# Small loads on GpSimd's queue, ten groups in flight, and gates kept in PSUM in a planned graph-network kernel

## The chip, the cores and the metric

The kernel runs on one core of a Trainium2 chip. Its time is the device time of one execution in microseconds (us), and the time before is the median of three runs. A core has five engines that run side by side, each with its own queue of instructions taken in order: TensorE (PE: matrix multiplication; PEld: its weight loads), VectorE (DVE), ScalarE (ACT), GpSimd (POOL) and SyncE (SP), which here only issues transfers (DMAs). SBUF is the working memory. PSUM is the memory that TensorE writes to, in eight banks of 128 partitions x 512 float32 numbers.

## The reference, cut to what matters

```
x: (64, 256, 128)    adj: (256, 256)    weights of 128 x 128 or multiples
x = layernorm(x + sum over k of adj^k x W0[k])       # layer 0: powers 0 to 3, each of two stacks
x = layernorm(x + adj (x W1) + b1)                   # layer 1
x = layernorm(x + norm(adj + I) x W2^T + b2)         # layer 2
h = x                                                # layer 3: a gated recurrence
for step in range(5):
    m  = adj h                                       # in and out matrices are both adj
    av = [m, m];  u = h U3^T + u3_b
    z  = sigmoid(av W3^T + w3_b + u)
    r  = sigmoid(av W4^T + w4_b + u)
    c  = tanh(av W5^T + w5_b + (r h) U5^T + u5_b)    # the candidate
    h  = (1 - z) h + z c                             # = h + z (c - h)
x = layernorm(x + h)
```

Every multiplication is float32.

## The kernel before, in words

The 64 batches are handled in 32 groups of two (`NB`). A group's data is a tile of 128 partitions x 512 numbers. Each group goes through the four layers as a long chain of small operations, and several groups are in flight at once, so that one group's matmuls run while others wait for VectorE, ScalarE, GpSimd or a DMA. Names in the profile are those of the values: `x`, `pmq`, `py` in layer 0; `pm`, `m`, `py`, `yb` in layers 1 and 2; and in step s of the recurrence `pmg`, `mg` (the product with adj), `pr` and `ph` (PSUM banks), `r`, `z`, `hv` (the gates and the candidate), `rh`, `d` = hv - hT, `e` = z d, `hT` (the new state, transposed). The state is then turned into `h` by a VectorE transpose (`th`) and a round trip through DRAM (`dh`, `h`). `pmg`, `pm` and `pmq` are multiplications of 256 x 256 blocks done with seven products instead of eight (`seven`): GpSimd makes the differences `ts` and `tq`, TensorE multiplies in four parts (first, middle, more, rest), ScalarE and VectorE add the blocks up.

Nothing of the order is written by hand. `record` of each group hands every operation to a `Plan`, with its engine, an estimated cost, a lag until the result can be used, and a rank. `Plan.order` then goes through time: on each engine it takes the operation that could start first, and among those that could start together the one of lowest rank. It also gives out the buffers: `slots` says how many there are of each kind (8 PSUM banks, 60 tiles of kind w, and so on), and a value gets a slot at its first use and gives it back after its last. What comes out is one fixed list of instructions for each engine. The rank of a group is its number; for the last `LEVEL` groups it grows with the number of operations the group has already recorded, so that they advance side by side. `ACTIVE` is the number of groups in flight: a group's first operation waits for the last operation of the group `ACTIVE` before it.

The first `HEAD` = 4 batches (two groups) turn x on TensorE (`ptx`), since nothing else is ready yet; the other groups turn it on VectorE (`tx`) and through DRAM (`dx`, `xT`). The last `END` = 8 batches (four groups) turn the final state back on TensorE (`pth`); the others on VectorE (`tn`) and through DRAM (`dn`, `hn`). Then comes the last layernorm: `s` (the sum), `st` and `mv` (statistics on VectorE), `ve`, `nm`, a power on GpSimd (`rs`), and the scaling `y` on ScalarE (lines 475 to 497 and 536 to 545), and the store.

Before the groups, `pre` and `load` (lines 214 to 221) add the operations that prepare constants: `ident` (an identity matrix made by GpSimd), 14 warm-up transposes on TensorE, the transpose and the square of adj, `w0s` (summed and centred by `w0m`), `wb` (the weight of layer 1 and the two biases, centred by `wbm`), the `s_` block sums, and `braw` and `bsum` (the biases of the recurrence). All their loads are issued on SP. The block sums and the centring run on VectorE ahead of the groups' first transposes of x.

The matmul helper is line 198, so every product and block product shows as L198 in the profile. The gates are line 691, the elementwise operations of the recurrence line 698.

Of the kernel before, what the change touches and what calls it, by code (L numbers as in the profile page):

```python
# [13 lines left out]
P = 128  # L14
NB = 2
ACTIVE = 8
HEAD = 4
LEVEL = 5
END = 8
STEPS = 5  # L20
# [136 lines left out]
def kernel(  # L157
# [39 lines left out]
    def mm(o, lhsT, rhs, start, stop, shared=False):  # L197
# [3 lines left out]
              "ve": [P, Q], "rs": [P, Q]}  # L201
    slots = {"bank": BANKS, "x": ACTIVE + 3, "w": 60, "th": 8, "q": 8, "dram1": 8, "dram2": 16, "st": 12, "mv": 12, "ve": 24, "rs": 12}
    plan = Plan(slots)
# [9 lines left out]

    def pre(rank, engine, cost, run, reads=(), writes=()):
        lag = {"SP": 2300, "PE": 260, "DVE": 260, "ACT": 130, "POOL": 100}[engine]
        plan.add(engine, cost, lag, rank, run, reads, writes)

    def load(rank, name, shape, src, keep=True):
        v = constant(name, shape) if keep else Val("w", shape, name)
        pre(rank, "SP", 450, lambda: nc.sync.dma_start(v.ap, src), [], [v])  # L220
        return v
# [140 lines left out]
    wb, wbm = constant("wb", [P, 3, C]), constant("wbm", [P, 3])  # L362
    pre(1.3, "SP", 450, lambda: nc.sync.dma_start(wb.ap[:, 0, :], w1), [], [wb])
    for i, b in ((1, b1), (2, b2)):
        pre(1.4, "SP", 450, lambda i=i, b=b: nc.sync.dma_start(
            wb.ap[:, i, :], bass.AP(tensor=b.tensor, offset=b.offset, ap=[[0, P], [1, C]])), [wb], [wb])
    pre(0.35, "DVE", 1100, lambda: centre(wb, wbm), [wb], [wb, wbm])
    w1c, b1c, b2c = ((wb, wb.ap[:, i, :]) for i in range(3))
    raw = {name: load(1.5, f"raw_{name}", [P, src.shape[1]], src, False)
           for name, src in (("w2", w2), ("w4", w4_w), ("w3", w3_w), ("w5", w5_w), ("u3", u3_w), ("u5", u5_w))}  # L370
# [29 lines left out]

    def biases():
        for i, src in enumerate((w3_b, w4_b, w5_b, u3_b, u3_b, u5_b)):
            nc.sync.dma_start(braw.ap[:, i:i + 1], src.rearrange("(p o) -> p o", o=1))

    pre(2.5, "SP", 2200, biases, [], [braw])
    pre(0.4, "DVE", 150, lambda: nc.vector.tensor_add(bsum.ap, braw.ap[:, :3], braw.ap[:, 3:]), [braw], [bsum])
# [26 lines left out]
    class Group:  # L433
# [33 lines left out]
        def act(self, run, reads, writes, cost=None, joint=False):  # L467
            return self.add("ACT", cost or act_cost(self.width), 130, run, reads, writes, joint)

# [4 lines left out]

        def statistics(self, tag, s):
            st, mv, ve, rs, nm = (self.val(k, n + tag) for k, n in (
                ("st", "st"), ("mv", "mv"), ("ve", "ve"), ("rs", "rs"), ("ve", "nm")))

            def stats():
                for q in range(self.q):  # L480
                    nc.vector.bn_stats(st.ap[:, q * 6:(q + 1) * 6], nat(s)[:, q, :])  # L481

            def aggr():
                for q in range(self.q):
                    nc.vector.bn_aggr(mv.ap[:, 2 * q:2 * q + 2], st.ap[:, q * 6:(q + 1) * 6])
                mean, var = (mv.ap.rearrange("p (q k) -> p k q", k=2)[:, k] for k in range(2))
                nc.vector.tensor_scalar(ve.ap, var, EPS, None, op0=OP.add)
                nc.vector.tensor_scalar(nm.ap, mean, -1.0, None, op0=OP.mult)

            def scales():  # L490
                nc.gpsimd.tensor_tensor(rs.ap, ve.ap, half[:, :self.q], op=OP.pow)
                nc.gpsimd.tensor_tensor(mv.ap[:, :self.q], nm.ap, rs.ap, op=OP.mult)

            self.dve(stats, [s], [st], 195 * self.q)
            self.dve(aggr, [st], [mv, ve, nm], 67 * self.q + 240)
            self.add("POOL", 1420, 100, scales, [ve, nm], [rs, mv])
            return mv, rs

        def spread_of(self, tag, s):

            y, ve, rs = self.val("w", "y" + tag), self.val("ve", "ve" + tag), self.val("rs", "rs" + tag)

            def squares():
                for q in range(self.q):
                    nc.scalar.activation(nat(y)[:, q, :], nat(s)[:, q, :], AF.Square, scale=C ** -0.5,  # L505
                                         accum_out=ve.ap[:, q:q + 1])

            def scales():
                nc.gpsimd.tensor_scalar(ve.ap, ve.ap, EPS, None, op0=OP.add)  # L509
                nc.gpsimd.tensor_tensor(rs.ap, ve.ap, half[:, :self.q], op=OP.pow)  # L510

            self.act(squares, [s], [y, ve], 400 * self.q)
            self.add("POOL", 1330, 100, scales, [ve], [ve, rs])
            return y, rs

        def normalise_centred(self, tag, s):
            y, rs = self.spread_of(tag, s)

            def run():
                for q in range(self.q):  # L520
                    nc.scalar.mul(nat(y)[:, q, :], nat(s)[:, q, :], rs.ap[:, q:q + 1])  # L521

            self.act(run, [s, rs], [y], 380 * self.q)
            return y
# [6 lines left out]
        def residual(self, tag, ps, resid, left=lambda v: v.ap, right=lambda v: v.ap):  # L531
            s = self.val("w", "s" + tag)
            self.dve(lambda: nc.vector.tensor_add(right(s), left(ps), right(resid)), [ps, resid], [s])
            return (s, *self.statistics(tag, s))

        def normalise(self, tag, s, mv, rs):
            y = self.val("w", "y" + tag)

            def run():
                for q in range(self.q):  # L540
                    nc.scalar.activation(nat(y)[:, q, :], nat(s)[:, q, :], AF.Identity, bias=mv.ap[:, q:q + 1],
                                         scale=rs.ap[:, q:q + 1])

            self.act(run, [s, mv, rs], [y], 400 * self.q)
            return y

        def propagate(self, tag, h, aTs, ins=None, blocks=False, fast=True):

            if fast and self.nb == 2:
                return self.seven(tag, h, aTs, ins or tiles, blocks)  # L550
            ps, outs = self.val("bank", "pm" + tag), by_block if blocks else None

            def run():
                o, a = (outs or plain)(ps), ins or tiles
                for b in range(self.nb):
                    for kt in range(T):
                        mm(o[b], a(h)[:, b, kt], aTs.ap[:, kt, :], kt == 0, kt == T - 1)

            self.pe(pe_cost(N, self.q), run, [h, aTs], [ps])
            return self.copied("m" + tag, ps)  # L560

        def seven(self, tag, h, aTs, ins, blocks):
# [60 lines left out]
            started = self.pe(pe_cost(P, 1), first, [h, aTs], [ps])  # L623
            kept = self.act(lambda: nc.scalar.copy(row(u, 1), row(ps, 0)), [ps], [u], act_cost(P))  # L624
            self.add("POOL", 830, 100, ts01, [h], [ts])
# [6 lines left out]
            self.dve(post13, [ps, w], [m], 215)  # L632
            self.act(lambda: nc.scalar.copy(o(m, 0), o(ps, 0, False)), [ps], [m], act_cost(P), True)
            self.pe(pe_cost(P, 2), rest, [h, tq, sums], [ps], True)
# [60 lines left out]

        def tensor(self, name, op, a, b, way=lambda v: v.ap, out=lambda v: v.ap):
            t = self.val("w", name)
            self.dve(lambda: nc.vector.tensor_tensor(out(t), way(a), way(b), op=op), [a, b], [t])  # L698
            return t

        def record(self):
            x_ = self.val("x", "x")
            plan.add("SP", 450, 4500 if self.start < HEAD else 2700, self.rank(), lambda: nc.sync.dma_start(nat(x_), self.view(x)), [], [x_],
                     self.load_gate)
# [24 lines left out]
            for t in range(T):  # L729
# [12 lines left out]
                self.pe(pe_cost(2 * C, 2 * self.nb), first, [xT, qT, w01, w0s], [p])  # L742
                self.act(moved, [p], [v], act_cost(self.nb * C))
            for t in range(T):
# [10 lines left out]
                self.pe(pe_cost(self.nb * C, T), second, [v, aT], [py[t]])  # L755
                self.act(summed, [py[t]], [s0], act_cost(self.nb * C))
            y = self.normalise_centred("0", s0)
# [24 lines left out]
            for s in range(STEPS):  # L782
# [8 lines left out]
                self.product(pr, w34T, m, False, True, shared=True)  # L791
                z = self.gate_(f"z{s}", pr, AF.Sigmoid, zb)
                self.product(ph, u5T, rh, False, True)
                hv = self.gate_(f"hv{s}", ph, AF.Tanh, hb)

                d = self.tensor(f"d{s}", OP.subtract, hv, hT)
                e = self.tensor(f"e{s}", OP.mult, z, d)
                if s < STEPS - 1:
# [79 lines left out]
```

## Time and profile before

| | |
|---|---|
| median of three runs | 1366.85 us (1366.57 to 1367.98) |
| the profiled run | 1367.95 us, span of its instructions 1365.1 us |
| PE, DVE, ACT, POOL busy | 98%, 72%, 56%, 55% of the span |
| granted TensorE clock | 0.997 of full speed |
| DMA | 134.42 MB, 98 GB/s on average |
| x load, issue to landing (median) | 3.2 us |

The profile is one execution recorded by the hardware. A page gives each engine's busy time, the chain of work that ended last (followed back from the last instruction), and the costliest groups of equal instructions. A row of a group reads: line, engine, operation, written tile <- read tiles, shapes, count | busy us in all, mean ns of one | idle time of the engine just before these instructions, and what ended it. A row in order of time reads: start us, length us, engine, line, operation, tiles, count. A float32 product appears as two matmul records.

### The profile page before, as it was taken

Reading aid. Unit: us, or ns where it says so; the run is one execution under the profiler, and the core shown is the slowest. Engines: PE = TensorE matmul, PEld = TensorE weight load, DVE = VectorE, ACT = ScalarE, POOL = GpSimd, SP = SyncE. Lnnn points to the kernel's source line nnn. Section 1 sums busy time; section 2 is a strip of 40 time slices with the busy share of each in tenths; the row PEclk is TensorE's granted clock in tenths of the full one; section 3 lists DMA queues with packets and bytes.
Section 4 is the critical chain, followed back from the end, with each engine's and each line's share of the span. In section 5 each row is a group of like instructions: output and inputs, shape, how many; then the busy total and the mean of one; then the engine's idle time right before and its main releaser. Section 6 shows DMA issues by size and latency. Waiting matters only on the chain.

```text
span 1365.1 us, 21963 instructions
## 1 busy us (share of the span) xinstructions
PE 1335.7 (98%) x6517; PEld 923.9 (68%) x6517; DVE 983.1 (72%) x2335; ACT 763.7 (56%) x2406; POOL 747.0 (55%) x1089
## 2 busy tenths in 40 slices
PE   8999999999999999999999999999999999999996
PEld 7986756677676666677767666766677766755553
DVE  5466777767767877776767777776766776878777
ACT  3675555555655545565565555654656556754444
POOL 3785643464765455555774554654665446843222
PEclk9999999999999999999999999999999999999998
DMA  6222233442334334333332333232433223233232
GB/s 171 63 63 71 84 101 109 123 117 84 96 93 117 98 96 124 109 95 100 109 101 78 109 118 107 86 106 80 129 101 96 85 86 93 88 114 109 79 93 60
DMA packets 269670, 134.42 MB, mean 98 GB/s; under 512 B 176368, under 2 KB 241392, under 8 KB 269552
## 3 DMA queue, kind: packets, MB, share of 16 engines
q1 hardware_dynamic: 269552, 133.03, 33.7%
q8 instruction: 52, 0.85, 0.3%
q14 instruction: 66, 0.54, 0.1%
HBM read 67.05 MB, written 65.54 MB: 97 GB/s over the span
## 4 chain that ended last, share of the span: by engine, by line
PE 89%; DVE 5%; DMA 2%; ACT 1%; issue 1%; POOL 1%; SPq 1%; ACTq 0%; POOLq 0%; DVEq 0%
PE pr L198 28%; PE ph L198 19%; PE pmg L198 18%; PE py L198 15%; PE pm L198 6%; PE pmq L198 3%; DMA x<-in_x_dram 1%; DVE hT L698 1%; DVE d L698 1%; DVE e L698 0%; DMA w_raw<-in_L_gnn_weight_dram 0%; DVE th L672 0%; DVE rh L698 0%; DVE st L481 0%; DMA wb<-in_L_gnn_b_dram 0%
## 5 line engine op out<-in xcount | busy, mean ns | idle before, releaser
L198 PE MATMUL pr<-mg,w435u5T 128*128 128x512 f32 x640 | 323.5, 595 | 2.0 <-ACT r L691 1.4
L583 POOL TENSOR_TENSOR tsg<-h 128x256 f32<-128x256 f32 x128 | 106.9, 835 | 222.4 <-DMA h<-dh 138.6
L691 ACT ACTIVATE r<-pr,bsum 128x512 f32<-128x512 f32 x160 | 109.6, 685 | 151.3 <-PE pr L198 148.1
L698 DVE TENSOR_TENSOR rh<-r,hT 128x512 f32<-128x512 f32 x160 | 123.2, 770 | 77.4 <-ACT r L691 76.8
L691 ACT ACTIVATE z<-pr,bsum 128x512 f32<-128x512 f32 x160 | 109.7, 685 | 107.7 <-PE pr L198 104.4
L698 DVE TENSOR_TENSOR d<-hv,hT 128x512 f32<-128x512 f32 x160 | 118.1, 738 | 69.5 <-ACT hv L691 68.5
L198 PE MATMUL ph<-rh,w435u5T 128*128 128x512 f32 x320 | 163.9, 595 | 1.1 <-DVE rh L698 1.1
L198 PE MATMUL ph<-mg,w435u5T 128*128 128x512 f32 x320 | 163.3, 592 | 0.0
L198 PE MATMUL pr<-hT,w2u3T 128*128 128x512 f32 x320 | 162.7, 592 | 0.0
L198 PEld LDWEIGHTS pr<-mg,w435u5T 128*128 128x128 f32 x640 | 107.1, 191 | 56.2 <-issue 38.2
L691 ACT ACTIVATE hv<-ph,bsum 128x512 f32<-128x512 f32 x160 | 109.4, 685 | 43.3 <-PE ph L198 42.7
L521 ACT ACTIVATE y<-s,rs 128x128 f32<-128x128 f32 x384 | 122.2, 393 | 13.7 <-POOL rs L510 13.3
L505 ACT ACTIVATE y<-s 128x128 f32<-128x128 f32 x384 | 113.8, 302 | 25.5 <-DVE s L528 25.3
L198 PEld LDWEIGHTS pmg<-s_aTp,tsg 128*128 128x128 f32 x768 | 102.8, 191 | 37.2 <-issue 31.1
L698 DVE TENSOR_TENSOR hT<-hT,e 128x512 f32<-128x512 f32 x160 | 123.7, 773 | 1.4
L698 DVE TENSOR_TENSOR e<-z,d 128x512 f32<-128x512 f32 x160 | 121.4, 759 | 1.9
L198 PEld LDWEIGHTS pmg<-aTp,h 128*128 128x128 f32 x512 | 88.2, 197 | 46.6 <-issue 34.9
L621 DVE TENSOR_TENSOR mg<-pmg,usg 128x256 f32<-128x256 f32 x160 | 67.1, 419 | 62.8 <-PE pmg L198 59.5
L198 PE MATMUL pmg<-s_aTp,tsg 128*128 128x128 f32 x768 | 106.6, 275 | 1.2 <-ACT usg L624 1.0
L510 POOL TENSOR_TENSOR rs<-ve,half 128x4 f32<-128x4 f32 x96 | 101.9, 1062 | 8.0
L509 POOL TENSOR_SCALAR ve<-ve 128x4 f32<-128x4 f32 x96 | 24.5, 255 | 141.8 <-ACT y L505 141.8
L198 PEld LDWEIGHTS ph<-mg,w435u5T 128*128 128x128 f32 x320 | 58.7, 190 | 63.6 <-issue 48.5
(170 smaller groups left out, 2846.9 us busy)
## 6 DMA issues: line engine op xcount, KB each, us to landing
dh<-th SPq DMA_DIRECT2D x160, 256.0 KB, 2.0
h<-dh SPq DMA_DIRECT2D x256, 128.0 KB, 2.5
x<-in_x_dram SPq DMA_DIRECT2D x32, 256.0 KB, 3.2
hT<-dh SPq DMA_DIRECT2D x128, 64.0 KB, 2.0
out_dram<-y SPq DMA_DIRECT2D x32, 256.0 KB, 2.4
dx<-tx SPq DMA_DIRECT2D x30, 256.0 KB, 2.5
xT<-dx SPq DMA_DIRECT2D x60, 128.0 KB, 2.6
dn<-tn SPq DMA_DIRECT2D x28, 256.0 KB, 2.0
```

The source lines that it names most:

```text
L198: nc.tensor.matmul(o, lhsT, rhs, start=start, stop=stop, skip_group_check=shared)
L505: nc.scalar.activation(nat(y)[:, q, :], nat(s)[:, q, :], AF.Square, scale=C ** -0.5, accum_out=ve.ap[:, q:q + 1])
L509: nc.gpsimd.tensor_scalar(ve.ap, ve.ap, EPS, None, op0=OP.add)
L510: nc.gpsimd.tensor_tensor(rs.ap, ve.ap, half[:, :self.q], op=OP.pow)
L521: nc.scalar.mul(nat(y)[:, q, :], nat(s)[:, q, :], rs.ap[:, q:q + 1])
L583: nc.gpsimd.tensor_tensor(ts.ap[:, :2 * P].rearrange("p (x c) -> p x c", x=2), ins(h)[:, 1], ins(h)[:, :, 0], op=OP.subtract)
L621: nc.vector.tensor_tensor(o(m, slice(1, 3)), o(ps, slice(1, 3), False), both, op=OP.add)
L691: self.act(lambda: nc.scalar.activation(t.ap, ps.ap, func, bias=bias[1], scale=1.0), [ps, bias[0]], [t], act_cost(self.width) + 100)
L698: self.dve(lambda: nc.vector.tensor_tensor(out(t), way(a), way(b), op=op), [a, b], [t])
```

## The change

It has five parts.

- The loads of the two biases in `wb` and the six of `braw` are issued from GpSimd's queue; the loads of `w1` and the raw weights stay on SP, at an earlier rank. Loads into one tile no longer wait for each other (`joint`). x is loaded at the rank of a group one and a half places earlier.
- `ACTIVE` goes from 8 to 10, with more slots of the kinds w, th and q; `LEVEL` from 5 to 7.
- `END` goes from 8 to 4, so two groups rather than four turn their state back on TensorE; these two scale the last layernorm on VectorE instead of ScalarE, without the negated mean.
- z and the candidate are written by ScalarE over their own PSUM banks (`pr`, `ph`), and z times the difference by VectorE over z.
- The estimated costs and lags of ScalarE's operations (and a few others) that the planner uses are changed.

```diff
-ACTIVE = 8
+ACTIVE = 10
-LEVEL = 5
-END = 8
+LEVEL = 7
+PLAIN = 0
+END = 4
...
-    slots = {"bank": BANKS, "x": ACTIVE + 3, "w": 60, "th": 8, "q": 8, ...
+    slots = {"bank": BANKS, "x": ACTIVE + 3, "w": 64, "th": 10, "q": 10, ...
...
+    def fetch(rank, o, src, v, queue):
+        e, cost = QUEUES[queue]
+        pre(rank, queue, cost, lambda: e.dma_start(o, src), [], [v], lag=3000, joint=True)
...
-    pre(1.3, "SP", 450, lambda: nc.sync.dma_start(wb.ap[:, 0, :], w1), [], [wb])
+    fetch(0.1, wb.ap[:, 0, :], w1, wb, "SP")
     for i, b in ((1, b1), (2, b2)):
-        pre(1.4, "SP", 450, lambda i=i, b=b: nc.sync.dma_start(
-            wb.ap[:, i, :], bass.AP(tensor=b.tensor, offset=b.offset, ap=[[0, P], [1, C]])), [wb], [wb])
+        fetch(0.1, wb.ap[:, i, :], bass.AP(tensor=b.tensor, offset=b.offset, ap=[[0, P], [1, C]]), wb, "POOL")
...
-    pre(2.5, "SP", 2200, biases, [], [braw])
+    for i, src in enumerate((w3_b, w4_b, w5_b, u3_b, u3_b, u5_b)):
+        fetch(0.2, braw.ap[:, i:i + 1], src.rearrange("(p o) -> p o", o=1), braw, "POOL")
...
-            return self.add("ACT", cost or act_cost(self.width), 130, run, reads, writes, joint)
+            return self.add("ACT", cost or act_cost(self.width), 190, run, reads, writes, joint)
...
+            def near():
+                for q in range(self.q):
+                    nc.vector.tensor_scalar(nat(y)[:, q, :], nat(s)[:, q, :], mv.ap[:, 2 * q:2 * q + 1],
+                                            rs.ap[:, q:q + 1], op0=OP.subtract, op1=OP.mult)
...
-            self.act(run, [s, mv, rs], [y], 400 * self.q)
+            if self.start >= B - END:
+                self.dve(near, [s, mv, rs], [y], 257 * self.q)
+            else:
+                self.act(run, [s, mv, rs], [y], 390 * self.q)
...
-            plan.add("SP", 450, 4500 if self.start < HEAD else 2700, self.rank(), ...
+            plan.add("SP", 450, 4500 if self.start < HEAD else 2700, self.rank() - 1.5, ...
...
-                z = self.gate_(f"z{s}", pr, AF.Sigmoid, zb)
+                z = self.gate_(f"z{s}", pr, AF.Sigmoid, zb, False)
...
-                hv = self.gate_(f"hv{s}", ph, AF.Tanh, hb)
+                hv = self.gate_(f"hv{s}", ph, AF.Tanh, hb, False)
...
-                e = self.tensor(f"e{s}", OP.mult, z, d)
+                e = self.tensor(f"e{s}", OP.mult, z, d, into=pr)
```

## The prediction

> **What bounds the kernel now**
>
> I read the page first (busy shares and the chain that ended last), then the busy time by stage, then the groups of instructions, then the rows in order of time where TensorE is not full: the start and the end.
>
> ```profile
> span 1365.1 us, 21963 instructions
> PE 1335.7 (98%) x6517; PEld 923.9 (68%) x6517; DVE 983.1 (72%) x2335; ACT 763.7 (56%) x2406; POOL 747.0 (55%) x1089
> ...
> PE 89%; DVE 5%; DMA 2%; ACT 1%; issue 1%; POOL 1%; SPq 1%; ACTq 0%; POOLq 0%; DVEq 0%
> ```
>
> TensorE is the bound: 98% busy and 89% of the chain. But the ends of its records are modelled, so I also price its work by the spacing of its starts when it runs densely. In the rows in order of time the median spacing is 0.4295 us for a record of 512 columns, 0.216 for 256 and 0.112 for 128. The groups hold 1600, 792 and 4125 such records: 687.2 + 171.1 + 462.0 = 1320.3 us. So 1365.1 - 1320.3 = 44.8 us of the span are not TensorE's work. The stages say where they lie (columns: window, its length, then busy time and instruction count of each engine):
>
> ```profile
> 0.00:40.00 40.00, 33.23 (x187) 29.72 (x188) 19.93 (x65) 16.50 (x55) 15.20 (x30) 1.00 0.65 179
> 40.00:100.00 60.00, 60.00 (x386) 52.64 (x385) 31.77 (x78) 42.09 (x190) 50.77 (x80) 1.00 0.15 43
> 100.00:1300.00 1200.00, 1190.35 (x5746) 812.44 (x5745) 884.18 (x2064) 674.85 (x2101) 663.12 (x952) 1.00 0.35 100
> 1300.00:1340.00 40.00, 40.00 (x166) 23.92 (x165) 30.29 (x62) 17.46 (x35) 10.38 (x19) 1.00 0.30 86
> 1340.00:1366.00 26.00, 12.12 (x40) 5.19 (x38) 16.89 (x67) 12.81 (x27) 7.49 (x10) 0.83 0.18 51
> ```
>
> Summing (start to next start, less the dense spacing) over each stage gives: head, to 40 us, 8.6 and 1.3 before the first matmul; middle, 40 to 1340, 20.2; from 1340 to TensorE's last record 6.0; after it 8.4. They make 44.5, and the rest is rounding. The head's largest part is three waits for x (columns: start, length, engine, line):
>
> ```profile
> 17.46 1.23 SPq L703 DMA_DIRECT2D x<-in_x_dram  x1
> ...
> 25.98 0.46 PE L198 MATMUL pmq<-a2T,x 128*128 128x128 f32 x2 [2.06 <-DMA x<-in_x_dram]
> ...
> 32.39 0.49 PE L198 MATMUL pmq<-a2T,x 128*128 128x128 f32 x2 [0.65 <-DMA x<-in_x_dram]
> 34.53 0.46 PE L198 MATMUL pmq<-a2T,x 128*128 128x128 f32 x2 [1.65 <-DMA x<-in_x_dram]
> ```
>
> The middle's 20.2 us are some 40 short waits, mostly for ScalarE or VectorE results that come a few tenths late. The end is VectorE's: it works almost without a pause from 1349.4 to 1358.9, and after its last row come GpSimd's power, four ScalarE rows and the store.
>
> ```profile
> 1349.96 0.68 DVE L698 TENSOR_TENSOR rh<-r,hT 128x512 f32<-128x512 f32 x1
> ...
> 1358.70 0.17 DVE L488 TENSOR_SCALAR nm<-mv 128x4 f32<-128x4 f32 x1
> ...
> 1360.19 1.65 ACT L541 ACTIVATE y<-s,mv,rs 128x128 f32<-128x128 f32 x4 [0.81 <-POOL mv L492]
> ```
>
> **What the Trainium skill says**
>
> SBUF — State Buffer, "Who interferes with whom": a VectorE instruction with two SBUF inputs and a GpSimd instruction that reads SBUF lock each other out for a whole instruction; with one SBUF input at most it doesn't. The trace agrees:
>
> ```profile
> L698 DVE TENSOR_TENSOR hT<-hT,e 128x512 f32<-128x512 f32 x160 | 123.7, 773 | 1.4
> L698 DVE TENSOR_TENSOR e<-z,d 128x512 f32<-128x512 f32 x160 | 121.4, 759 | 1.9
> L698 DVE TENSOR_TENSOR d<-hv,hT 128x512 f32<-128x512 f32 x160 | 118.1, 738 | 69.5 <-ACT hv L691 68.5
> L528 DVE TENSOR_TENSOR s<-py,yb 128x512 f32<-128x512 f32 x64 | 43.5, 682 | 12.6 <-PE py L198 11.4 <-POOL ts L587 1.1
> ```
>
> The row with a PSUM input takes 682 ns; the three with two SBUF inputs take 738 to 773, though the median of their rows, read one by one, is 690: the mean is raised by a minority that is held up.
>
> ScalarE: Activation LUTs, "Step-by-step: what each stage is for": ScalarE writes PSUM faster than SBUF. No ScalarE row here writes PSUM.
>
> PSUM — Partial Sum Buffer, "Summary: rules for kernel authors": evacuate promptly, since PSUM is tight. The kernel uses all eight banks.
>
> DMA: Bandwidth & Descriptors, "Specifications": first byte about 1 us from GpSimd's queue, 0.6 from SP's. No GpSimd DMA is in this trace.
>
> **The change part by part**
>
> *Head.* Eight loads (two of wb, six of braw) leave SP for GpSimd's queue; they took 1.28 + 1.38 + 0.43 + 0.58 = 3.7 us of SP's issue. The load of b2 stood behind w0p, so wbm waited 3.2 us for it on VectorE with the transposes of x behind it; x_4 and x_6 were issued only at 17.46. Now they go ahead of w0p, and wbm's 1.3 us of VectorE work comes before w0m. From w0_raw's landing (7.75, now some 0.5 later because x_2 is issued first) VectorE has 9.3 us of work to the end of s_aTp, plus wbm 1.3: tx_4 starts at about 18.9 instead of 21.56. The chain tx_4, dx_4, x_8 moves 2.7 us earlier: x_8's wait of 2.1 goes, x_12's 0.7 too. x_14 lands 2.7 earlier, but TensorE asks for it 2.9 earlier too, so its wait stays near 1.8. Gain 2.9. On GpSimd, eight issues of about 1 us (the page's price, an estimate) precede dinv, which slips from 5.4 to about 9.5; ahat's rows on VectorE, moved behind w0m, need it at 11.7. One issue stands ahead of ident, so the 14 warm-up transposes (3.0 us) and p_at start up to 1 us later; TensorE waited 1.1 us for ahat at 9.36, and p_an now stands behind pmq_0, which absorbs that. If GpSimd's issues are slower, the gain drops to 0; if x_14 comes in time, it is 4.5.
>
> *Middle.* Ten groups instead of eight, truer costs, and buffers for them (w 64, th and q 10) only reorder. I counted, in the written order of both programs, how much TensorE work lies between a matmul and the later one that needs its result through another engine. Shares of tight links fall: product to product through one gate of ScalarE, 22 of 160 under 1.2 us before and 3 after; the last block matmul to the product through post2, 20 under 1.0 before and 14 after; the minimum of that link goes from 0.45 to 0.86. The sum of what links lack against their latency falls from 17 to 8 us. The 17 is close to the 18.3 us of waits over 30 ns found in the trace, so I take 9 us off. The long links (gate to next step's h, 5% point 20.8 before, 21.6 after) are covered in both.
>
> *PSUM.* z, hv and e in PSUM give d, e and hT one SBUF input each: from 738, 759 and 773 to about 685, 160 times each, 34 us of VectorE time, all beside TensorE; its worth is in the 9 us. ScalarE's z and hv: gain 0 to 50 ns, I take 0. VectorE's write of e to PSUM has no row: nearest is the 682 of L528, bounds 650 and 750, I take 685. Against it: the bank of pr is now free after hT's add, not after z. From the last u5T matmul to that point the trace of before shows 0.17 plus 2.9 at least, 3.8 median, 5.75 at the 95% point. In the new order the next user of the bank comes 4.0 us of TensorE work later at the least, 4.5 at the 5% point, 6.7 median. That is mostly enough; the overlap costs an estimated 1 us (0 to 6). So the middle gives -8.
>
> *End.* END 4 leaves two groups on the direct path, so two more take the DMA path: two VectorE transposes more (0.70 each) and eight transposes fewer on TensorE (-0.9 us). Two groups normalise on VectorE: four rows of about 0.22 (nearest: L350) instead of 1.65 us on ScalarE, and lose nm and one GpSimd multiply. LEVEL 7 draws seven groups instead of five to the end together. At the spacings of the rows above (0.61 for 512 elements, 0.78 for st, 0.66 for a transpose), VectorE work from the last rh is 8.9 before and 13.4 after: y of group 60, s, st, mv of group 58 all stand there. After that before has 6.2 us to the end (power 1.0, multiply 0.2, ScalarE 1.65, store 3.2, hops), after has 1.1 of power plus 3.25 of store. So 17.75 against 15.1: +2.65. Earlier, from rh of the first of the seven to the last rh, VectorE has 34.7 us of work and TensorE 34.0, so both can't stay full; taking the larger of the two stretch by stretch gives 41, averaging gives 35. I take 38, that is 4 us of TensorE waits where before had 2.2: +1.85. End: +4.5 (+2 to +8).
>
> Sum: -0.9 - 2.9 - 8 + 4.5 = -7.3 on the profiled span. That run took 1367.95; the median 1366.85 is what I subtract from: 1359.6.
>
> **The rivals**
>
> *More gain.* Middle waits nearly close (-14), end +1.5, head -4.5: 1366.85 - 0.9 - 17.0 = 1349. For it: faster VectorE rows also shorten queues, which the link count leaves out. Against it: part of the 20.2 is jitter under 30 ns a row.
>
> *It cancels.* The middle's waits come from queues on VectorE, not from short links, so only 1 to 2 us go, while head and end go as above: 1366.85 - 0.9 - 2.9 - 1.5 + 4.5 = 1366. For it: VectorE is 72% busy in order.
>
> *Slower: the banks of pr and ph.* TensorE, in order, waits for hT's add (and d's read of ph) before its next group may start a bank. Each of 160 steps losing on average 0.125 us costs 20 us: 1359.6 + 1 + 20 - 9 = about 1372, counting the middle gain as lost. It decides from about 46 ns a step (7.3 us). For it: release latencies of 4.5 to 6 us happen in a quarter of the steps. Against it: the smallest distance, 4.0, is already above the latency's median.
>
> *The change doesn't do what it says.* If VectorE rows stay at 738 to 773, the reorder's gain remains; the result is 1 to 3 us worse.
>
> **How the numbers follow**
>
> A difference of 0.2% (2.7 us) is what a measurement of this kernel can tell from none. Forecast (1354 to 1364.1) 0.58; more gain 0.12; cancels (to 1369.6) 0.17; slower 0.13. Faster is 0.58 + 0.12 = 0.70. The range 1351 to 1369 leaves some 0.06 below and 0.14 above; the forecast's own is 1354 to 1364.
>
> **What would show it**
>
> Head: TensorE's waits for x before 40 us fall from 4.4 to about 1.8. PSUM: d, e, hT near 685 ns. Middle: TensorE idle from 100 to 1300 down from 9.7 to about 5. Banks: waits of TensorE's pm, pr or ph for VectorE's hT or d would be the slower rival. End: VectorE full for the last 45 us, its last row y, and over 15 us from the last rh to the end. I am wrong if VectorE's PSUM write is slow (over 750 ns), or if the end costs over 10 us.

## The result, and the profile after

The changed kernel takes 1358.16 us (median of four runs, 1357.06 to 1359.65); the kernel before took 1367.16 in the same measurement. The ratio is 0.9934, 95% interval 0.9917 to 0.9952: faster by 0.7%. That is 9.0 us less, where the prediction had 7.3, and 1.4 us below its 1359.6. The profiled run has a span of 1355.7 us at a granted clock of 0.996, against 1365.1 before.

The page of the changed kernel, its span, busy times and the engines' shares of the chain that ended last:

```profile
span 1355.7 us, 21892 instructions
...
PE 1331.2 (98%) x6509; PEld 922.0 (68%) x6509; DVE 953.2 (70%) x2343; ACT 756.0 (56%) x2398; POOL 678.0 (50%) x1095
...
PE 94%; DVE 3%; DMA 1%; issue 0%; ACT 0%; SPq 0%; POOL 0%; POOLq 0%; DVEq 0%; ACTq 0%
```

TensorE has 94% of the chain instead of 89%. VectorE has 30 us less to do, GpSimd 69 us less, although no instruction of GpSimd's arithmetic was taken out of the groups' steps. By stage (window, length, busy us and count of PE, PEld, DVE, ACT, POOL, then clock and DMA):

```profile
0.00:40.00 40.00, 34.16 (x189) 30.01 (x189) 21.39 (x65) 16.72 (x56) 21.41 (x41) 1.00 0.67 185
40.00:100.00 60.00, 59.90 (x390) 52.53 (x391) 29.81 (x79) 41.25 (x182) 49.74 (x80) 1.00 0.23 68
100.00:1300.00 1200.00, 1197.76 (x5797) 818.83 (x5796) 856.17 (x2062) 673.20 (x2112) 593.28 (x954) 1.00 0.34 99
1300.00:1340.00 40.00, 38.27 (x133) 19.90 (x131) 35.49 (x92) 20.76 (x41) 9.14 (x15) 1.00 0.35 107
1340.00:1356.00 16.00, 1.12 (x4) 0.71 (x4) 10.36 (x50) 4.10 (x10) 4.43 (x6) 0.63 0.30 85
```

From 100 to 1300 us TensorE is idle for 2.2 us; before it was 9.65. At the end the picture turns: after 1340 TensorE does almost nothing while VectorE works for 10 of 16 us.

The same ledger as in the prediction (each TensorE record's distance to the next, less the dense spacing of its size) gives, in us. "Slack" is what a distance has over the dense spacing. The middle reaches from 40 us to 36 us before the span's end:

| | before | after | difference | predicted |
|---|---|---|---|---|
| TensorE's work | 1320.2 | 1319.3 | -0.9 | -0.9 |
| ahead of the first matmul, and slack to 40 us | 1.3 + 8.6 | 2.5 + 6.8 | -0.6 | -2.9 |
| slack in the middle | 20.2 | 8.9 | -11.3 | -8 |
| slack in the last 36 us, and from the last TensorE record to the end | 6.0 + 8.7 | 8.3 + 9.8 | +3.4 | +4.5 |
| sum | | | -9.4 | -7.3 |

Half of what the middle gains, 5.6 us, lies in its last 220 us (256 to 36 us before the span's end): the slack there falls from 6.8 to 1.2.

In the page's groups the step's four 512-column VectorE rows read (busy us, mean ns, then the idle time before and its releaser):

```profile
L714 DVE TENSOR_TENSOR rh<-r,hT 128x512 f32<-128x512 f32 x160 | 125.5, 787 | 71.6 <-ACT r L707 67.5
...
L714 DVE TENSOR_TENSOR d<-ph,hT 128x512 f32<-128x512 f32 x160 | 109.8, 686 | 78.3 <-ACT ph L707 77.3
...
L714 DVE TENSOR_TENSOR pr<-pr,d 128x512 f32<-128x512 f32 x160 | 110.6, 692 | 1.5
...
L714 DVE TENSOR_TENSOR hT<-hT,pr 128x512 f32<-128x512 f32 x160 | 108.6, 680 | 1.7
```

d, e (now `pr`) and hT fell from 738, 759 and 773 ns to 686, 692 and 680. rh, which still reads two SBUF tiles, did not.

### The profile page after: what moved, and what is told of

The parts are those of the page before. It is cut to its first block, busy times and chain, and to the rows that moved or that the text cites. A ratio compares the mean times of both kernels' runs of the same rounds, so it can differ in the third digit from the quotient of the medians.

```text
span 1355.7 us, 21892 instructions
## 1 busy us (share of the span) xinstructions
PE 1331.2 (98%) x6509; PEld 922.0 (68%) x6509; DVE 953.2 (70%) x2343; ACT 756.0 (56%) x2398; POOL 678.0 (50%) x1095
## 4 chain that ended last, share of the span: by engine, by line
PE 94%; DVE 3%; DMA 1%; issue 0%; ACT 0%; SPq 0%; POOL 0%; POOLq 0%; DVEq 0%; ACTq 0%
PE pr L199 30%; PE ph L199 20%; PE pmg L199 18%; PE py L199 15%; PE pm L199 7%; PE pmq L199 3%; DMA x<-in_x_dram 1%; DMA w_raw<-in_L_gnn_weight_dram 1%; DVE st L487 0%; DMA dx<-tx 0%; DVE s L541 0%; DVE rh L714 0%; DVE tx L730 0%; ACT y L529 0%; DVE y L554 0%
## 5 line engine op out<-in xcount | busy, mean ns | idle before, releaser
L599 POOL TENSOR_TENSOR tsg<-h 128x256 f32<-128x256 f32 x128 | 96.4, 753 | 211.5 <-DMA h<-dh 145.0
L707 ACT ACTIVATE pr<-pr,bsum 128x512 f32<-128x512 f32 x160 | 105.6, 660 | 120.7 <-PE pr L199 115.9
L714 DVE TENSOR_TENSOR d<-ph,hT 128x512 f32<-128x512 f32 x160 | 109.8, 686 | 78.3 <-ACT ph L707 77.3
L707 ACT ACTIVATE ph<-ph,bsum 128x512 f32<-128x512 f32 x160 | 105.5, 659 | 63.7 <-PE ph L199 62.9
L529 ACT ACTIVATE y<-s,rs 128x128 f32<-128x128 f32 x384 | 122.1, 392 | 15.4 <-POOL rs L518 14.7
L517 POOL TENSOR_SCALAR ve<-ve 128x4 f32<-128x4 f32 x96 | 22.6, 235 | 214.3 <-ACT y L513 214.2
L513 ACT ACTIVATE y<-s 128x128 f32<-128x128 f32 x384 | 113.7, 301 | 18.4 <-DVE s L536 18.2
L714 DVE TENSOR_TENSOR pr<-pr,d 128x512 f32<-128x512 f32 x160 | 110.6, 692 | 1.5
L627 DVE TENSOR_TENSOR usg<-usg,pmg 128x128 f32<-128x128 f32 x160 | 45.2, 284 | 91.9 <-PE pmg L199 67.2
L714 DVE TENSOR_TENSOR hT<-hT,pr 128x512 f32<-128x512 f32 x160 | 108.6, 680 | 1.7
```

Source lines behind the costliest of these rows:

```text
L599: nc.gpsimd.tensor_tensor(ts.ap[:, :2 * P].rearrange("p (x c) -> p x c", x=2), ins(h)[:, 1], ins(h)[:, :, 0], op=OP.subtract)
L627: nc.vector.tensor_tensor(row(u, 0), row(u, 1), row(ps, 3), op=OP.add)
L707: self.act(lambda: nc.scalar.activation(t.ap, ps.ap, func, bias=bias[1], scale=1.0), [ps, bias[0]], [t], act_cost(self.width) + 100)
```

## The experiments

Each kernel was timed in turn with the kernel before, on one chip; e1 to e4, e5 to e8, e9 to e11 and e12 ran on different chips, so ratios are compared, and a loss or gain in us is the difference of ratios times 1367. Such a difference is uncertain by about 0.2%. The head, middle and end columns are the ledger of the one profiled run of each (head with the time ahead of the first matmul; end with the time after the last TensorE record). A profiled run can lie 2 us from its kernel's median: e5's is 1.9 us above, e3's 1.8, e4's and e8's 2.2 us below. "Lack" is the sum of what the tight links of the written order fall short of. It is a count made from the order that the planner writes, with ties between equally late inputs settled in one fixed way; no trace shows it. It puts the kernel before at 13.3 us and the changed one at 6.2, where the prediction's count said 17 and 8.

| | ratio to before, 95% interval | us | head | middle | end | lack |
|---|---|---|---|---|---|---|
| before | 1 | | 9.9 | 20.2 | 14.7 | 13.3 |
| changed | 0.9934, 0.9917 to 0.9952 | 1358.16 | 9.3 | 8.9 | 18.1 | 6.2 |
| e1 gates in SBUF, planned anew | 0.9962, 0.9949 to 0.9974 | 1361.23 | 9.5 | 13.2 | 17.4 | 5.2 |
| e2 before, with PSUM alone | 1.0024, 1.0014 to 1.0034 | 1369.91 | 10.3 | 22.6 | 14.5 | 17.6 |
| e3 eight groups | 0.9995, 0.9987 to 1.0003 | 1366.09 | 8.8 | 16.6 | 17.8 | 9.9 |
| e4 old costs | 0.9988, 0.9979 to 0.9996 | 1365.50 | 9.5 | 14.9 | 17.8 | 7.8 |
| e5 gates in SBUF, same order | 1.0010, 1.0004 to 1.0017 | 1368.40 | 11.6 | 19.5 | 18.2 | 6.2 |
| e6 old end | 0.9968, 0.9956 to 0.9981 | 1362.60 | 10.5 | 15.5 | 14.6 | 7.7 |
| e7 old head | 0.9930, 0.9916 to 0.9943 | 1358.51 | 11.1 | 8.6 | 17.4 | 6.2 |
| e8 a version from the pieces | 0.9930, 0.9918 to 0.9943 | 1357.92 | 9.3 | 10.2 | 14.7 | 5.6 |
| e9 two lags | 0.9915, 0.9903 to 0.9928 | 1355.74 | 9.5 | 7.1 | 17.8 | 0.5 |
| e10 e9, ident first, END 8 | 0.9905, 0.9892 to 0.9919 | 1354.97 | 10.2 | 7.8 | 15.5 | 0.5 |
| e11 e9 in SBUF, same order | 0.9978, 0.9968 to 0.9989 | 1364.29 | 10.6 | 14.7 | 17.8 | 0.5 |
| e12 r in PSUM too | 0.9907, 0.9890 to 0.9924 | 1355.26 | 11.3 | 6.5 | 16.2 | 1.6 |

Theory A is the prediction's: the order (ten groups, truer costs, more buffers) carries the middle's gain. B: the time freed on VectorE and GpSimd carries it. C: results that stay in PSUM hold the banks longer and are a burden.

**e1, e2: the PSUM part undone, and alone**

```diff
 e1, against the changed kernel:
-                z = self.gate_(f"z{s}", pr, AF.Sigmoid, zb, False)
+                z = self.gate_(f"z{s}", pr, AF.Sigmoid, zb)
-                hv = self.gate_(f"hv{s}", ph, AF.Tanh, hb, False)
+                hv = self.gate_(f"hv{s}", ph, AF.Tanh, hb)
-                e = self.tensor(f"e{s}", OP.mult, z, d, into=pr)
+                e = self.tensor(f"e{s}", OP.mult, z, d)
 e2: the same three lines the other way round, in the kernel before
```

> The changed kernel with z, the candidate and e put back into SBUF; all else stays. Theory A (the order carries the gain: ten groups, truer costs, more buffers): d, e and hT rise from 680-692 ns to 740-775, GpSimd's rows too, but TensorE's middle loses only 0 to 3 us, so 1358 to 1361 us. Theory B (the freed VectorE and GpSimd time carries it): the middle's slack goes from 9 back to about 20 us, 1368 us. Theory C (PSUM results hold the banks of pr and ph longer and are a burden that the ten groups pay for): the middle gets shorter by up to 4 us, 1354 to 1358; walking the written order with the durations of the traces gives an estimate of -3.6 us before any lock on VectorE is counted.

> The kernel before with only the PSUM part added; eight groups, the old costs, buffers, head and end stay. Theory A: d, e and hT fall to about 690 ns and the time falls a little, 1364 to 1367 us. Theory B: most of the middle's gain appears, 1356 to 1360. Theory C: the bank of pr is kept from w4T's product to hT's add, eight groups don't fill the time, and TensorE waits: walking the written order with the durations of the traces gives an estimate of +14 us over the kernel before, so about 1380; the profile would show middle idle of 20 us or more.

Without PSUM the changed kernel loses 0.28%, 3.8 us, of which the middle has 4.3: between A and B. PSUM alone makes the kernel before *slower* by 0.24%, though d, e and hT do fall to 677 to 692 ns. That excludes B by itself. C has the sign of e2 right but not the size (+3.3 us, not +14), and e1's sign wrong; and no wait of TensorE's `pr`, `ph` or `pm` for hT or d is in e2's list of waits. What rises in e2 is the lack of the links, 13.3 to 17.6. The likely reason is that a bank comes free later, so that the planner finds a worse order.

**e3, e4: eight groups, old costs**

```diff
 e3:
-ACTIVE = 10
+ACTIVE = 8
-... "w": 64, "th": 10, "q": 10, ...
+... "w": 60, "th": 8, "q": 8, ...
 e4 (some of nine such places):
-            return self.add("ACT", cost or act_cost(self.width), 190, run, ...
+            return self.add("ACT", cost or act_cost(self.width), 130, run, ...
-            self.act(squares, [s], [y, ve], 295 * self.q)
+            self.act(squares, [s], [y, ve], 400 * self.q)
```

> The changed kernel with eight groups in flight and the old numbers of buffers (w 60, th 8, q 8); PSUM, costs, head and end stay. Theory A: the tight links come back, the middle's slack goes from 9 to 15 to 18 us: 1364 to 1368 us. Theory B: nothing changes, 1357 to 1360. Theory C: eight groups can't cover the longer bank times; the estimate from the written order is +20 us over the changed kernel: about 1378.

> The changed kernel, planned with the old durations and the old ScalarE lag of 130 ns; ten groups, PSUM, head and end stay. Theory A: part of the tight links comes back (product to product through one gate), the middle's slack rises by 2 to 5 us: 1360 to 1363 us. Theory B: no change, 1357 to 1360. Theory C: little change, the estimate from the written order is +1.7 us: 1358 to 1361.

Each takes most of the gain away: e3 loses 0.61% (8.3 us), e4 0.54% (7.4 us), more than any theory gave e4; e3 is as theory A had it. Together with e1 the single losses sum to 19.5 us, where the whole change gained 9: the parts need each other. C's +20 for e3 is refuted; the walk through the written order that I used for it overrates waits for banks and is not a measure to rely on.

**e5: PSUM undone, the order kept**

```diff
-            t = self.val("w", name) if kept else ps
-            self.act(lambda: nc.scalar.activation(t.ap, ps.ap, func, ...), [ps, bias[0]], [t], ...)
+            v = self.val("w", name)
+            t = v if kept else ps
+            t.held = v
+            self.act(lambda: nc.scalar.activation(v.ap, ps.ap, func, ...), [ps, bias[0]], [t, v], ...)
 (and tensor() reads and writes the held tiles in the same way)
```

The planner still believes that the banks are held, so every queue has the same instructions in the same order (the two traces agree); only the places of z, the candidate and e differ.

> The changed kernel in its own written order, instruction for instruction, but z, the candidate and e are written to SBUF. e1 changed the order as well; here only the places of the data differ. If PSUM acts by the lock between VectorE and GpSimd (theory B's part), d, e and hT rise to about 760-780 ns and the middle's slack goes from 8.9 to 12 to 16 us: 1361 to 1365 us. If PSUM acted mainly through the order that the planner finds (theory A), the time stays at 1357 to 1359.5. If PSUM holds TensorE up through the banks (theory C), giving the banks back early makes it faster: 1354 to 1357.

This is the run that moved my view. It is slower than the changed kernel by 0.76%, 10.4 us: the whole gain is gone, more than the 3 to 7 us that were expected of the lock. The middle's slack is back at 19.5 us. The groups show where it comes from:

```profile
L718 DVE TENSOR_TENSOR rh<-r,hT 128x512 f32<-128x512 f32 x160 | 128.2, 804 | 68.0 <-ACT r L709 64.1
...
L718 DVE TENSOR_TENSOR d<-hv,hT 128x512 f32<-128x512 f32 x160 | 120.9, 756 | 71.8 <-ACT hv L709 69.6
...
L718 DVE TENSOR_TENSOR hT<-hT,e 128x512 f32<-128x512 f32 x160 | 125.5, 785 | 1.7
...
L718 DVE TENSOR_TENSOR e<-z,d 128x512 f32<-128x512 f32 x160 | 125.3, 784 | 1.6
```

and in the 1200 us of the middle VectorE is busy 33 us more than in the changed kernel's row above, GpSimd 70 us more:

```profile
100.00:1300.00 1200.00, 1191.92 (x5769) 814.47 (x5768) 889.65 (x2048) 672.84 (x2104) 663.52 (x953) 1.00 0.34 98
```

The means hide what happens. Read row by row, the medians of all four rows are 691 to 693 ns. Of their 640 rows, 261 lie beside no tensor instruction of GpSimd, and none of these lasts 750 ns. Of the 379 that overlap one, 194 last 750 ns or more, the longest 1802. In the changed kernel 254 rows of d, e and hT overlap GpSimd, and the longest takes 700 ns. This is what the Trainium skill's page SBUF — State Buffer, "Who interferes with whom", describes, a lock for a whole instruction when VectorE reads two SBUF inputs, and this pair of traces agrees.

TensorE seldom waits for d, e or hT. It waits for rh, and for mg and m, which stand behind the held rows on VectorE. From the lists of waits (who waited, for whom: us in all, times, longest), first the changed kernel, then e5:

```profile
PE ph L199 <- DVE rh L714: 0.7, 2, 0.5
PE pmg L199 <- DVE mg L633: 0.5, 1, 0.5
...
PE pmg L199 <- DVE mg L633: 1.6, 2, 1.0
PE ph L199 <- DVE rh L718: 1.3, 4, 0.6
PE pr L199 <- DVE mg L637: 1.2, 2, 0.9
```

In the middle the waits listed for VectorE grow from 1.4 to 4.8 us, those for ScalarE from 0.9 to 2.7, and none names d, e or hT. So the held rows act through the queue. e5 also gives back ScalarE's 25 ns on each z and candidate (below); no run separates the two, but VectorE's waits grow more.

**e6: the old end**

```diff
-LEVEL = 7
-END = 4
+LEVEL = 5
+END = 8
-            if self.start >= B - END:      # normalise on VectorE
+            if False:
```

> The changed kernel with the end of before: LEVEL 5, END 8, normalisation on ScalarE in all groups. The prediction's step for the end (+4.5, measured +3.3 between the two traces, less 0.9 for the transposes that come back to TensorE): 1358.2 - 3.3 + 0.9 = 1355.8, plus up to 1.5 us because the middle's order changes with LEVEL: 1355 to 1358. From the last rh to the end some 15 us instead of 18.9. Rival (the two ends are worth the same, the difference of the traces came from how the groups before happened to lie): 1358 to 1360.

Its last 36 us did what was expected: 14.6 us instead of 18.1. The last rh stands at

```profile
1345.78 0.68 DVE L714 TENSOR_TENSOR rh<-r,hT 128x512 f32<-128x512 f32 x1
```

15.1 us before the span's end of 1360.8. But the kernel is slower than the changed one by 4.6 us, since the middle went from 8.9 to 15.5. Up to 873 us TensorE has the changed kernel's instructions in the same order, with the same slack (5.1 us from 40 us on, against 5.2). All that is added comes later, where the edit begins to act; one stretch holds 3.5 us of idle TensorE:

```profile
1000.00:1200.00 200.00, 196.52 (x970) 136.83 (x969) 136.21 (x340) 118.17 (x399) 103.47 (x165) 0.99 0.29 87
```

From 256 to 36 us before the span's end the slack is 8.6 us, against 1.2 in the changed kernel. The kernels before and e2, also with LEVEL 5 and END 8, have 6.8 and 6.1 there. The nine with LEVEL 7 have 0.8 to 3.3, and e10, whose END is 8 too, has 0.8; e8 (LEVEL 5) has 4.0 and e12 (LEVEL 6) 3.0. So the end's part of the change costs 3.5 us in the last 36 and gives back more ahead of them, and the comparison points to LEVEL as what does the latter. No run changes LEVEL alone.

**e7: the old head**

```diff
-    fetch(0.1, wb.ap[:, 0, :], w1, wb, "SP")
+    pre(1.3, "SP", 450, lambda: nc.sync.dma_start(wb.ap[:, 0, :], w1), [], [wb])
... (the loads of b1, b2, the raw weights and braw likewise as before; all on SP)
-            plan.add("SP", 450, 4500 if self.start < HEAD else 2700, self.rank() - 1.5, ...
+            plan.add("SP", 450, 4500 if self.start < HEAD else 2700, self.rank(), ...
```

> The changed kernel with the loads of before: all small loads on SP, in the old places, and x without its lead of 1.5 in rank. The prediction's step for the head (-2.9): undoing it gives 1361. The difference measured between the traces (-0.6: 1.8 less waiting, 1.2 more ahead of the first matmul): 1358 to 1359.5. A rival says that GpSimd's eight loads are a net loss, since they stand ahead of the identity matrix: 1355 to 1358; then the first matmul starts at 1.3 us instead of 2.5 and TensorE's slack up to 40 us stays below 9.3 in total.

No difference: 0.9930 against 0.9934. The waits for x come back, and the first matmul starts earlier:

```profile
1.34 3.25 PE L247 MATMUL warm<-ident 128*128 128x128 f32 x14 [1.34 <-POOL ident masks.py:199]
...
25.68 0.46 PE L199 MATMUL pmq<-a2T,x 128*128 128x128 f32 x2 [1.96 <-DMA x<-in_x_dram]
...
32.65 0.49 PE L199 MATMUL pmq<-a2T,x 128*128 128x128 f32 x2 [0.98 <-DMA x<-in_x_dram]
...
34.19 0.68 PE L199 MATMUL pmq<-a2T,x 128*128 128x128 f32 x4 [1.06 <-DMA x<-in_x_dram]
```

Its profiled head is 11.1 us, the changed kernel's 9.3. Runs that share the changed kernel's loads spread from 8.8 (e3) to 11.6 (e5), so one profile doesn't tell a microsecond here. The time says that the head's part of the change is worth nothing that can be measured.

**e8: a version from the pieces**

```diff
-    make_identity(nc, ident)              # ahead of the planned part
+        make_identity(nc, ident)          # first thing in the written order, ahead of the loads
-LEVEL = 7
-END = 4
+LEVEL = 5
+END = 6
-            return self.add("ACT", ..., 190, ...
+            return self.add("ACT", ..., 240, ...
```

(The last two groups normalise on VectorE, as in the changed kernel.)

> A version meant to beat both: the changed kernel with the identity matrix made ahead of GpSimd's loads (first matmul at 1.3 instead of 2.5 us), LEVEL 5 with END 6 and VectorE's normalisation in the last two groups, and a ScalarE lag of 240 ns in the planner. By the sums: head -1.2, end -2 to -3, middle within 2 us of the changed kernel either way: 1352 to 1356 us. If the middle's order matters more than what it is planned with (a change of one lag moves it by several us by chance), 1356 to 1361.

1357.92: level with the changed kernel, and in the range of the second theory, not of the sums. The first matmul starts at 1.35 us and the end has 14.7, as wanted, but the middle has 10.2 us of slack instead of 8.9; the profiled run, with a span of 1354.0, was this kernel's fastest.

**e9 to e11: the links**

If the links set the middle, an order with little lack should be faster. e9 takes two lags at which the count finds almost none.

```diff
 e9:
-            return self.add("DVE", cost or dve_cost(self.width), 260, run, ...
+            return self.add("DVE", cost or dve_cost(self.width), 270, run, ...
-            return self.add("ACT", cost or act_cost(self.width), 190, run, ...
+            return self.add("ACT", cost or act_cost(self.width), 280, run, ...
 e10: e9, ident as in e8, and
-END = 4
+END = 8                                   # the last two groups still normalise on VectorE
 e11: e9 with e5's edit
```

> The changed kernel with two numbers of the planner changed: the time it allows from a ScalarE result to its user 280 ns instead of 190, from a VectorE result 270 instead of 260. No instruction is added or removed, only the order changes. Counted as in the prediction, the links from one matmul to the next one that needs its result lack 0.5 us in sum instead of 6 (a recount that puts the kernel before at 13, the changed one at 6, e3 at 10, e4 at 8, e6 at 8; their measured middle slack was 20.2, 8.9, 16.6, 14.9, 15.5). If the tight links set the middle: its slack falls from 8.9 to 2 to 6 us, 1351 to 1355. If what is left is queues and jitter: 1357 to 1360. If each new order is a draw that the count doesn't foresee: 1360 to 1366.

> e9's two lags, the identity matrix made ahead of GpSimd's loads, and END 8 with LEVEL 7 (the last four groups take the direct path with its eight more transposes on TensorE, the last two normalise on VectorE). By the sums: head -1.2, end -2, transposes +0.9 against e9: 1349 to 1353 if the links set the middle; 1355 to 1358 if they don't.

> e9 in its own written order, but z, the candidate and e in SBUF, as e5 was to the changed kernel. e5 lost 10.6 us of middle slack through d, e and hT at 756-785 ns instead of 680-692. If the slower VectorE rows cost time only where a link is tight, e9's loose links hide them: 0 to 4 us over e9. If they cost it by queues on VectorE whatever the links, again some 10 us over e9.

e9 stands 0.19% (2.6 us) below the changed kernel, within the uncertainty of such a difference; only the order differs. Its middle has 7.1 us of slack. Both lie just above the range of the first theory (1351 to 1355 us, slack 2 to 6): the lack fell by 5.7 us, the slack by 1.8. A floor is left that the links don't explain.

```profile
100.00:1300.00 1200.00, 1198.43 (x5800) 820.34 (x5800) 849.00 (x2055) 669.19 (x2100) 587.77 (x959) 1.00 0.34 99
```

e10 has the lowest time here, 1354.97, but its step from e9, 0.1%, is below what can be told. It falls at the edge of the range for "the links don't set the middle". Its interval (0.9892 to 0.9919) and that of the changed kernel (0.9917 to 0.9952) just touch.

e11 loses 0.63%, 8.6 us, against e9: nearly as much as e5 lost, with almost no tight link in the order. Of its 640 rows 200 last 750 ns or more. So loose links hide little of what the held VectorE rows cost.

Put side by side, the slack of the kernels with PSUM gates goes roughly with the lack: e9 has 0.5 of lack and 7.1 of slack, e12 1.6 and 6.5, e8 5.6 and 10.2, the changed kernel 6.2 and 8.9, e6 7.7 and 15.5, e4 7.8 and 14.9, e3 9.9 and 16.6, e2 17.6 and 22.6. Part of that is the stretch ahead of the end seen in e6. Three kernels with SBUF gates stand above them at the same lack: by 7.6 us at 0.5 (e11), by 10.6 at 6.2 (e5), by 3 or 4 at 5.2 (e1). So held rows cost something beside short links.

But they are not a fixed sum on top. The kernel before has SBUF gates too, and with 13.3 of lack and 20.2 of slack it lies only about 1 us above the line from e3 to e2. Yet 162 of its 640 rows last 750 ns or more. e1 has 197 of them, as many as e5 (194), and loses much less. What held rows cost depends on the order: 8.6 and 10.4 us in two orders planned for PSUM gates, 3.8 when the planner knows of SBUF gates, about 1, by that line, in the order of before. Why is not shown.

**e12: r in PSUM too**

```diff
-                r = self.gate_(f"r{s}", pr, AF.Sigmoid, rb)
+                ph = self.val("bank", f"ph{s}")
+                r = self.gate_(f"r{s}", pr, AF.Sigmoid, rb, into=ph)
                 rh = self.tensor(f"rh{s}", OP.mult, r, hT)
-                ph = self.val("bank", f"ph{s}")
```

> A last try for a faster version, against e10: r goes to PSUM too, into the bank of ph ahead of w5T's product, so that rh, the last of the step's four 512-column VectorE rows with two SBUF inputs (745 to 800 ns), has one. The order was planned anew: lags 300 for TensorE and VectorE and 200 for ScalarE, LEVEL 6, END 6, all normalising on ScalarE, the identity matrix ahead of GpSimd's loads; the links lack 1.6 us in sum. If PSUM inputs are worth what e5 and e11 showed (8 to 10 us for three rows of a step), a fourth row gives 1 to 3 more: rh at 685 to 700 ns, GpSimd's rows shorter, 1351 to 1355 us. If holding ph's bank from r on and w5T's product waiting for rh cost more, TensorE waits for rh in the middle: 1356 to 1362.

```profile
L712 DVE TENSOR_TENSOR rh<-ph,hT 128x512 f32<-128x512 f32 x160 | 109.2, 683 | 38.3 <-ACT ph L705 38.0
```

rh falls to 683 ns, with none held up any more, and the middle has the least slack of all runs, 6.5 us. The time, 0.9907, is e10's, just above the range expected of a gain. Lags, LEVEL and END differ as well, and all groups normalise on ScalarE, so this run doesn't price the step alone.

## Why the prediction was right, and where its steps were off

The total fits better than its terms: the head gained 2.3 us less than predicted, the middle 3.3 more, and the end cost 1.1 less. That these partly cancel is luck.

**TensorE's work, -0.9**: as counted.

**Head, -2.9; measured -0.6, and by e7 nothing in the time.** The wanted effect came: waits for x fell from 4.4 to 1.6 us, where the prediction said 1.8. Three terms were missed or mis-sized. (The prediction's three x terms also come to 2.6, not 2.9.) These rows show them (a load issued on GpSimd ahead of ident; ident; the first matmul; w0_raw's landing; raw_u's; the first tx):

```profile
1.28 0.77 POOL L224 DMA_DIRECT2D wb<-in_L_gnn_bias_dram  x1 [0.34 <-issue]
2.15 0.31 POOL masks.py:199 TENSOR_SCALAR_AFFINE_SELECT ident<-ident 128x128 f32<-128x128 f32 x1
...
2.52 3.25 PE L247 MATMUL warm<-ident 128*128 128x128 f32 x14 [2.52 <-POOL ident masks.py:199]
...
9.41 0.40 DVE L287 TENSOR_TENSOR w0s<-w_raw,ident 128x128 f32<-128x128 f32 x1 [3.86 <-DMA w_raw<-in_L_gnn_weight_dram]
...
11.67 0.33 PE L397 MATMUL p_w2u3T<-ident,raw_u 128*128 128x128 f32 x1 [1.24 <-DMA raw_u<-in_L_gnn_u_w_dram]
...
21.22 1.30 DVE L730 STREAM_TRANSPOSE tx<-x 128x512 f32<-128x512 f32 x2
```

Ident came 1.2 us late. As predicted, the wait for ahat that went away made this good: p_w2u3T starts at 9.97, before at 10.00, with as much work done. What undid it is a wait for raw_u, 1.24 us, that was in nobody's account. w0_raw was used at 9.41, 1.66 us later than before and not 0.5: its load was issued 0.55 later, as taken, but needed 7.1 us to land instead of 6.0. Two loads of x now stand directly ahead of it; that they slow it is likely and not tested. From there to tx_4 VectorE takes 11.8 us and not 10.6. The earlier x lets GpSimd start on its differences at 15.19, beside VectorE's block sums, and some rows that took 0.28 us before are now longer, one of `s_aT` 0.81. So tx_4 starts at 21.22, not at 18.9. GpSimd's issues went the other way: the 1 us taken for each is a time to the first byte, used as if it were the engine's; they held it for 0.53 to 0.77 us, and dinv came at 6.17 instead of 9.5.

**Middle, -8; measured -11.3.** The sign is right, the reason half right. (The waits over 30 ns that make the 18.3 us are 76 in the ledger, not some 40.) The prediction took 9 us off for the links and let the PSUM part's worth be "in the 9 us". That term fails: at an unchanged order PSUM is worth 10.4 us (e5 against the changed kernel) and 8.6 (e11 against e9), and still 3.8 when the planner may answer (e1). PSUM also has a price that the prediction put down as waits for banks, 1 us: those waits aren't there (none in the changed kernel's list, single ones of 0.5 us in e3's and e4's), the price seems to be a worse order, and the eight groups and old costs of before can't pay it (e2: the lack rises by 4.3 us, the time by 0.24%). With ten groups and truer costs the same edit gains. Together the parts take 11 us off the middle; undone one by one, PSUM, ten groups and costs lose 3.8, 8.3 and 7.4. The prediction also booked LEVEL 7 at the end alone, as a cost of 1.85 us. As e6 shows, the end's part lowers the slack ahead of it, and 5.6 of the middle's 11.3 us lie there.

**PSUM rows**: 686, 692 and 680 ns for the 685 taken; e's write to PSUM, the unknown, 692. ScalarE's gain, taken as 0 in a range to 50, was 25 ns: 685 to 660 for z and 659 for the candidate. The Trainium skill's page ScalarE: Activation LUTs, "Step-by-step: what each stage is for", says that writes to PSUM are the faster ones; this case agrees.

**End, +4.5; measured +3.4, and -3.5 when undone (e6).** The mechanism is the predicted one: a queue on VectorE behind the last rh.

```profile
1336.75 0.68 DVE L714 TENSOR_TENSOR rh<-r,hT 128x512 f32<-128x512 f32 x1
...
1345.12 1.12 PE L659 MATMUL pth<-ident,hT 128*128 128x128 f32 x4 [5.64 <-DVE hT L714]
...
1350.53 1.12 DVE L554 TENSOR_SCALAR y<-s,mv,rs 128x128 f32<-128x128 f32 x4 [1.12 <-POOL rs L498]
```

From the last rh to the end it is 18.9 us; the prediction said 17.75, before it was 15.1. TensorE's last transposes wait 5.64 us for hT, whose d, e and add stand among other groups' statistics. The four VectorE rows of y take 1.12 us in all, some 0.28 each, not 0.22, and from the last of them to the end it is 4.0 us, not 3.25. Against that the stretch ahead of the last rh, taken as a cost of 1.85, cost nothing (3.4 in all, less the 3.8 behind the last rh).

**The rivals.** "Slower: the banks" didn't happen as a wait; as a worse order it is e2. Its sum also takes off the 9 us of the middle that it counts as lost. "It cancels" is refuted in its size by the middle; but its mechanism, queues on VectorE, is what e5 and e11 show. "More gain" had the middle 2.7 us too large, the forecast 3.3 too small, and it was wrong on head and end. That the change doesn't do what it says is refuted: the rows fell.

What stays open: the floor of about 7 us that the middle keeps in e9, e10 and e12, 2 us of it gaps under 30 ns; what LEVEL does alone; why held rows cost so little in the order of before; and how much of a new order is chance.

## What to carry to other kernels

Where VectorE and GpSimd work side by side, look at VectorE's longest rows and not at the median: here the medians of the step's rows stayed between 678 and 693 ns. A PSUM input ended the held rows in every run that had one. What that is worth hangs on the order: 8.6 and 10.4 us with the order fixed, 3.8 when the planner could answer, and a loss of 3.3 where it was the only edit. So pay for the bank: keep more work in flight and plan anew. When a planner writes the order, hold the order fixed if the edit itself is to be priced. And find where the two orders part before a stage is judged by itself: what was meant for the end acted from 873 us on.

## What the runs showed of the hardware

- A VectorE row of 0.69 us can take up to 1.8 us while GpSimd works; GpSimd's rows suffer too: its 256-column difference (`tsg`, 128 of them) takes 847 ns on average in e5, 753 in the changed kernel and 734 in e12, with the same instructions.
- A load issued from GpSimd's queue held GpSimd for 0.53 to 0.77 us, less than the 1 us taken as an estimate.
- In the runs with PSUM gates no d, e or hT row lasted over 700 ns, with or without GpSimd beside it.
- VectorE's product of a PSUM tile into the same PSUM tile takes 692 ns, the same as with SBUF tiles when nothing disturbs it (median 691).
